# Cross attention of two transformer blocks: weights divided before or after the product, and the mask as a matmul or as an addition

## The chip, the cores and the metric

The kernel runs on one core of one Trainium2 chip. A core has five engines with queues of their own: TensorE (PE; PEld is its loading of weights), VectorE (DVE), ScalarE (ACT), GpSimd (POOL) and SyncE (SP, which issues most DMAs here). The metric is the device time of one execution in microseconds (us), lower is better. TensorE writes to PSUM, of which the kernel has eight banks of 128x512 float32; VectorE and ScalarE read it, and in this kernel GpSimd works on SBUF alone.

## What is computed

Two transformer blocks in float32, one after the other, on x of shape (2, 1024, 256), with a context of (2, 64, 256): 16 heads of 16, so the scores of the self attention are 1024 x 1024 per head and batch and those of the cross attention 1024 x 64. Block 0 ends in a mixture of eight experts of which each token takes two; block 1 ends in a plain feed-forward layer. Cut to what matters here:

```python
def _mha(q_in, kv_in, ...):                       # block 0, self and cross
    scores = jnp.einsum('bhqd,bhkd->bhqk', q, k) / jnp.sqrt(jnp.float32(dh))
    attn = jax.nn.softmax(scores, axis=-1)
    out = jnp.einsum('bhqk,bhkd->bhqd', attn, v)
...
# block 1, cross attention
attn = jnp.einsum('bhnd,bhmd->bhnm', q, k) * SCALE
bias = (1.0 - codebook_mask.astype(attn.dtype))[:, None, None, :] * -10000.0
attn = jax.nn.softmax(attn + bias, axis=-1)
ca = _merge(jnp.einsum('bhnm,bhmd->bhnd', attn, v)) @ ca_proj_w.T
```

Only block 1's cross attention has a mask. Blocks are called layers below.

## The kernel before

**The loop.** Self attention (`self_attention`, one call per layer) works head group by head group: a *cell* is one of 128 steps, with four heads at once on TensorE's four row groups. In a cell it makes four "a" scores (L805) whose row maxima VectorE reduces from PSUM (L812), ten cells ahead (`LEAD`), four "b" scores (L816) whose exponentials ScalarE writes to SBUF (L822), and, for cells one or two back, the product with the values (L867). Its result is copied by ScalarE (L876, L879) and added up by GpSimd (L880). With 128 cells and ten ahead, the maxima stop at cell 118; `maxima[0]` says whether they still run, and `helper()` gives GpSimd while they do and VectorE after.

**The planner.** Everything else is written as Python generators, run by `Stream`. A generator gives out instructions and yields: a positive number is a step's planned TensorE time, a number of zero or less a pause (0.0: until the next cell; -1.5: at least 1.5 us, rounded up to cells of `CELL` = 2.9 us). After each cell the loop takes steps as long as the planned time that is owed allows (`RATE`: 2.5 us a cell in layer 0, 1.1 in layer 1, more where deadlines ask for it). After the last cell `rest` runs what is left, by rank and by the pauses. So the order of each engine's queue is fixed when the program is built: what a step gives out stands in each queue behind the cell's own work.

**The cross attention.** Each layer has four *units* of 512 rows (n = 0 to 3). A unit becomes available when the self attention of its rows is projected, every 32 cells. It is normalised (`norm`), weighed (`weigh`), and then added to x (`share`). Unit n waits for unit n - 1. `weigh` first projects the queries (L1113, L1120). Then, for two halves g of the heads with four score tiles r each (a tile is 128 rows of 8 blocks of 64 keys):

- `scores(g, n)` makes two tiles in two banks (L1143). In layer 1 a matmul of one row, ones by the mask, opens each sum (L1134).
- While the maxima run, ScalarE copies the tile to SBUF (L1154), and later steps `largest` reduce the eight maxima on VectorE (L1163) and subtract them on GpSimd (L1164). After the maxima VectorE does both at once, from PSUM.
- `weights_turned` transposes two tiles (L1179), and ScalarE takes the exponential on the way out of PSUM (L1183).
- `product(g)` multiplies by the values (L1192), sums each head's exponentials with 16 small matmuls (L1202), copies the product to `q` (L1209) and inverts the sums (L1211).
- `divided(g)` spreads the inverses with four matmuls (L1217) and multiplies (L1224).

Which of two step lists a unit follows is read from `maxima[0]` once, after the query projection (L1230). The lists differ in the pauses.

In layer 0 a unit is followed by `dispatch_task`, which chooses experts on VectorE and sends rows with 8 indirect DMAs from GpSimd; the experts' slots (`Mixture`) run after the loop, from 650 to 890 us. In layer 1 units 0 and 1 are followed by `forward_norm`, and the feed-forward tasks run after the loop.

**Constants.** `picks` (768 columns) holds the 0/1 matrices of the sums: `O_SUM` has four blocks of 32 columns, one for each r.

Of the kernel before, what the change touches and what calls it, by code (L numbers as in the profile page):

```python
# [50 lines left out]
P = 128  # L51
# [52 lines left out]
NCOL = 139  # L104


O_SUM, O_HEAD = 0, 128

O_ROWS, O_PART = 640, 704
NPICK = 768  # L110

W_O, W_V, W_Q, W_K = 0, 512, 1024, 1536
NSELF = 2048
# [88 lines left out]
def two_blocks(  # L202
# [323 lines left out]
    def self_attention(layer, tail, heads, arrive, extra, when_ready, beside=None):  # L526
# [224 lines left out]
        def side_by_side(parts, dst):  # L751

            i, o = bank()
            j, s = bank()
            for half, part in enumerate(parts):
                nc.tensor.matmul(
                    o[64 * half : 64 * (half + 1), :], lhsT=picks[:, O_ROWS : O_ROWS + 64],
                    rhs=part, start=True, stop=True,
                )
            for half, part in enumerate(parts):  # L760
                for c in range(4):
                    nc.tensor.matmul(
                        s[32 * c : 32 * (c + 1), :P],
                        lhsT=picks[:, O_PART + 32 * half : O_PART + 32 * (half + 1)],
                        rhs=part[:, c * P : (c + 1) * P],
                        start=(half == 0),
                        stop=(half == 1),
                    )
            inv = small.tile([P, P], F32, tag="inv", name=f"inv_{names}", bufs=1)
            nc.vector.reciprocal(inv, s[:, :P])  # L770
            nc.scalar.copy(dst, o)
            free.extend((j, i))
            yield 1.5
            yield -1.6
            i, by = bank()
            for c in range(4):
                nc.tensor.matmul(
                    by[:, c * P : (c + 1) * P],
                    lhsT=picks[:, O_HEAD + c * P : O_HEAD + (c + 1) * P],
                    rhs=inv, start=True, stop=True,  # L780
                )
            nc.vector.tensor_tensor(dst, dst, by, ALU.mult)
            free.append(i)
            yield 0.55
            yield -1.0
# [72 lines left out]
        def product(cells):  # L858

            h = cells[0] // 8  # L860
            b, g = h // 8, h % 4
            for cell in cells:
                stream.until(("values", b, cell % 8 & 6))
            n, o = bank()
            for cell in cells:
                for j in range(4):
                    nc.tensor.matmul(  # L867
                        o[32 * j : 32 * j + VW, :],
                        lhsT=V[b][:, cell % 8, 4 * g + j, :],
                        rhs=exps.pop((cell, j)),  # L870
                        start=(cell == cells[0]),
                        stop=(cell == cells[-1]),
                    )
            if cells[0] % 8 == 0:
                acc[h] = opool.tile([P, 512], F32, tag="acc", name=f"acc_{names}{h}")
                nc.scalar.copy(acc[h], o)  # L876
            else:
                part = opool.tile([P, 512], F32, tag="part", name=f"part_{names}{cells[0]}")
                nc.scalar.copy(part, o)  # L879
                helper().tensor_tensor(acc[h], acc[h], part, ALU.add)  # L880
            free.append(n)
            if cells[-1] % 8 == TB - 1:
                at_cell(cells[-1] + 3, lambda: finish(h, cells[-1] + 3))
# [219 lines left out]
    def weigh(layer, b, pool, w, name, held):  # L1103
# [21 lines left out]
        shape = [P, 4 * 2, SK]  # L1125
        less, pts, whole_scores = {}, {}, set()

        def scores(g, n):

            got = [(r, *bank()) for r in (2 * n, 2 * n + 1)]  # L1130
            for t in range(4):
                for r, _, p in got if layer == 1 else ():
                    at = slice(32 * r, 32 * r + 1)
                    nc.tensor.matmul(  # L1134
                        p[:, t * P : (t + 1) * P].rearrange("p (u k) -> p u k", k=SK),
                        lhsT=ones[at, :],
                        rhs=mask_f[at, b * SK : (b + 1) * SK].unsqueeze(1).to_broadcast([1, 2, SK]),
                        start=True,
                        stop=False,
                    )  # L1140
                for r, _, p in got:
                    rows = slice(32 * r, 32 * r + 32)
                    nc.tensor.matmul(  # L1143
                        p[:, t * P : (t + 1) * P],
                        lhsT=q[rows, g, t * P : (t + 1) * P],
                        rhs=kbd[rows, g, b].rearrange("p u k -> p (u k)"),
                        start=(layer == 0),
                        stop=True,
                    )
            for r, i, p in got:  # L1150
                sc = less[g, r] = pool.tile([P, 512], F32, tag="sc", name=f"sc_{name}{g}{r}", bufs=4)
                if maxima[0]:

                    nc.scalar.copy(sc, p)  # L1154
                    whole_scores.add((g, r))
                else:
                    subtract(sc, p, nc.vector, f"{g}{r}")
                free.append(i)

        def subtract(sc, src, engine, tag):  # L1160
            src = src.rearrange("p (c k) -> p c k", k=SK)
# [4 lines left out]
                mx.unsqueeze(2).to_broadcast(shape), ALU.subtract,  # L1166
            )

        def largest(g, r):
            if (g, r) in whole_scores:  # L1170
                subtract(less[g, r], less[g, r], nc.gpsimd, f"{g}{r}")

        def weights_turned(g, n):

            for r in (2 * n, 2 * n + 1):
                i, p = bank()
                sc = less.pop((g, r))
                for t in range(4):
                    nc.tensor.transpose(  # L1179
                        p[:, t * P : (t + 1) * P], sc[:, t * P : (t + 1) * P], ident  # L1180
                    )
                pt = pts[g, r] = pool.tile([P, 512], F32, tag="p1", name=f"pt_{name}{g}{r}", bufs=4)
                nc.scalar.activation(pt, p, AF.Exp, scale=SCALE)  # L1183
                free.append(i)


        inverse = {}

        def product(g):
            i, o = bank()  # L1190
            for r in range(4):
                nc.tensor.matmul(  # L1192
# [7 lines left out]
            for r in range(4):  # L1200
                for c in range(4):
                    nc.tensor.matmul(  # L1202
                        s[32 * c : 32 * (c + 1), :P],
                        lhsT=picks[:, O_SUM + 32 * r : O_SUM + 32 * (r + 1)],
                        rhs=pts[g, r][:, c * P : (c + 1) * P],
                        start=(r == 0),
                        stop=(r == 3),
                    )
            nc.scalar.copy(q[:, g, :], o)  # L1209
            inv = inverse[g] = pool.tile([P, P], F32, tag="inv", name=f"inv_{name}{g}", bufs=2)  # L1210
            nc.vector.reciprocal(inv, s[:, :P])  # L1211
            free.extend((i, j))

        def divided(g):
            i, p = bank()
            for c in range(4):
                nc.tensor.matmul(  # L1217
# [6 lines left out]
            nc.vector.tensor_tensor(q[:, g, :], q[:, g, :], p, ALU.mult)  # L1224
            free.append(i)

        held.update(ot=q, divided=divided)
        cost = 1.9 if layer else 1.0
        SC, LA, TU, PR, DI = scores, largest, weights_turned, product, divided
        if maxima[0]:  # L1230

            for now, wait in (
                (((SC, 0, 0), (LA, 0, 0)), 0.0),
                (((LA, 0, 1),), 0.0),
                (((SC, 0, 1), (LA, 0, 2)), 0.0),
                (((TU, 0, 0), (LA, 0, 3)), 0.0),
                (((SC, 1, 0), (LA, 1, 0)), 0.0),
                (((TU, 0, 1), (LA, 1, 1)), 0.0),
                (((SC, 1, 1), (LA, 1, 2)), 0.0),
                (((PR, 0), (LA, 1, 3)), -1.5),  # L1240
                (((TU, 1, 0),), None),
                (((DI, 0), (TU, 1, 1)), -1.4),
                (((PR, 1),), None),
            ):
                for step, *args in now:
                    step(*args)
                us = sum({SC: cost, TU: 1.15, PR: 1.1, DI: 0.55}.get(step[0], 0.0) for step in now)
                if us:
                    yield us
                if maxima[0]:  # L1250
                    yield 0.0
                elif wait is not None:
                    yield wait
            return
        for step, *args, wait in (
            (SC, 0, 0, None),
# [1 line left out]
            (TU, 0, 0, None),  # L1258
            (SC, 1, 0, None),
            (TU, 0, 1, -1.3),  # L1260
            (PR, 0, None),
            (SC, 1, 1, None),
            (TU, 1, 0, None),
            (DI, 0, None),
            (TU, 1, 1, -1.6),
            (PR, 1, None),
        ):
            step(*args)
            yield {SC: cost, TU: 1.15, PR: 1.1, DI: 0.55}[step]
            if wait:  # L1270
                yield wait

    def share(w, name, first, held):

        yield -2.6
        held["divided"](1)
        yield 0.55
        yield -1.2
        for t0 in range(0, 4, 2):
            yield from project_task(held["ot"], w, first + t0, t0, 2)  # L1280
# [732 lines left out]
def _layout(inputs):  # L2013
# [81 lines left out]
    cols[:E, C_RB] = l0["router_b"]  # L2095

    picks = np.zeros((P, NPICK), f32)
    for r in range(4):
        for u in range(2):
            for c in range(4):  # L2100
                picks[SK * u : SK * (u + 1), O_SUM + 32 * r + 8 * c + 2 * r + u] = 1.0
    for j in range(4):
        for d in range(DH):
            picks[32 * j + d, O_ROWS + DH * j + d] = 1.0
# [49 lines left out]
```

## Time and profile before

| | |
|---|---|
| median of 4 runs | 1614.35 us (1608.72 to 1615.77) |
| the profiled execution | 1607.04 us, span 1605.3 us |
| granted TensorE clock, mean | 0.991 |
| maxima of layer 0 (L805) | 22.7 to 544.9 us, cells to about 585 us |
| maxima of layer 1 | 900.3 to 1406.5 us, cells to about 1446 us |
| query projections of the units, layer 0 (L1113) | from 247.2, 379.8, 523.6 and 616.4 us |
| query projections of the units, layer 1 | from 1146.4, 1300.6, 1421.8 and 1483.9 us |
| tiles copied at L1154 / reduced from PSUM at L1163 | 38 / 26 |

Busy time by stretch, in us, from the view of windows:

| stretch | us | PE | DVE | ACT | POOL |
|---|---|---|---|---|---|
| loop of layer 0, 64 to 545 | 481.0 | 473.8 | 364.4 | 336.4 | 168.3 |
| loop of layer 1, 947 to 1406.5 | 459.5 | 455.4 | 343.2 | 325.3 | 132.4 |
| last cells of layer 1, 1407 to 1446 | 39.0 | 36.9 | 18.6 | 31.5 | 6.3 |
| end, 1446 to 1601 | 155.0 | 153.9 | 44.3 | 43.1 | 10.9 |

How to read the lines further below: a line of the timeline is start, duration, engine, line of the program, operation, what it writes from what, shapes, and how many instructions are merged; a float32 matmul is two instructions. In square brackets stands idle time of that engine before, and what ended it. Matmuls are pipelined, so a time on TensorE is best taken from one start to the next.

### The profile page before, as it was taken

To read this page: it belongs to the slowest core of one execution; us is meant where nothing else is said; L and a number is where in the kernel's file an instruction comes from. 1 tells how busy PE (TensorE), PEld (TensorE's weight loads), DVE (VectorE), ACT (ScalarE), POOL (GpSimd) and SP (SyncE) were. 2 spreads that over 40 slices of the span, in tenths; PEclk is the share of its full clock that TensorE was granted. 3 is DMA by queue.
4 is the path that set the end of the run, shared out by engine and by line. 5 is a ranking of instruction groups with operands and counts; after the bars stand their busy time and mean duration, and the time that the engine had idled before them with its cause. 6 is when DMAs were issued, how large, how long until landed. Compare 5 with 4: busy or idle time off the path is not lost. (4 is left out here: it accounts for less than half of the span.)

```text
span 1605.3 us, 28322 instructions
## 1 busy us (share of the span) xinstructions
PE 1569.6 (98%) x10710; PEld 874.3 (54%) x10710; DVE 982.5 (61%) x2094; ACT 914.5 (57%) x1770; POOL 411.0 (26%) x546
## 2 busy tenths in 40 slices
PE   7999999999998999999999999999999999999998
PEld 4433444544543547888888653344444445446766
DVE  6787766677779647611114558876767767845400
ACT  3487767666666755333223338876776676684321
POOL 2243323135235203411112033411222322311000
PEclk9899999999999999999999999999999999999999
DMA  5235311101000115375656320101110002000000
GB/s 162 111 135 202 106 28 35 28 21 48 15 21 35 55 50 198 117 276 197 201 185 209 89 83 18 35 22 24 31 41 15 22 14 84 22 8 21 14 13 27
DMA packets 55752, 121.07 MB, mean 75 GB/s; under 512 B 12219, under 2 KB 26429, under 8 KB 55229
## 3 DMA queue, kind: packets, MB, share of 16 engines
q1 hardware_dynamic: 51772, 109.07, 21.0%
q0 software_dynamic: 3456, 9.51, 1.6%
q8 instruction: 86, 1.41, 0.3%
q10 hardware_dynamic: 384, 0.66, 0.2%
q14 instruction: 54, 0.43, 0.1%
HBM read 71.68 MB, written 38.88 MB: 69 GB/s over the span
## 5 line engine op out<-in xcount | busy, mean ns | idle before, releaser
L812 DVE TENSOR_REDUCE mx_s<-banks 128x1 f32<-128x512 f32 x1024 | 634.1, 681 | 204.8 <-PE banks L805 203.0
L822 ACT ACTIVATE pt_s<-banks 128x512 f32<-128x512 f32 x1024 | 532.8, 609 | 156.9 <-PE banks L805 123.5
L805 PE MATMUL banks<-KS,QS 16*128 16x512 f32 x2048 | 533.6, 629 | 2.9 <-ACT part_s L879 1.4
L816 PE MATMUL banks<-qb_s,KS 32*128 32x512 f32 x2048 | 516.0, 621 | 7.4 <-DVE qb_s L715 3.6
L880 POOL TENSOR_TENSOR acc_s<-acc_s,part_s 128x512 f32<-128x512 f32 x141 | 179.4, 1272 | 433.0 <-ACT part_s L879 432.2
L816 PEld LDWEIGHTS banks<-qb_s,KS 32*128 32x128 f32 x2048 | 180.6, 186 | 179.4 <-DVE mx_s L812 107.1
L867 PE MATMUL banks<-pt_s,v_s 128*20 128x512 f32 x2048 | 262.1, 603 | 1.5 <-DVE mx_s L812 1.0
L805 PEld LDWEIGHTS banks<-KS,QS 16*128 16x128 f32 x2048 | 200.2, 185 | 70.5 <-issue 32.5
L867 PEld LDWEIGHTS banks<-pt_s,v_s 128*20 128x20 f32 x2048 | 43.1, 99 | 185.0 <-ACT pt_s L822 129.4
L1686 PE MATMUL banks<-w_slot,h_s 128*128 128x256 f32 x640 | 143.1, 380 | 0.0
L1686 PEld LDWEIGHTS banks<-w_slot,h_s 128*128 128x128 f32 x640 | 120.6, 190 | 19.7 <-DVE mx_s L812 1.5
L879 ACT COPY part_s<-banks 128x512 f32<-128x512 f32 x155 | 92.7, 598 | 61.0 <-PE banks L867 51.6
L1695 DVE SCALAR_TENSOR_TENSOR ys<-banks,gate,b 128x256 f32<-128x256 f32 x40 | 19.3, 483 | 162.1 <-PE banks L1686 160.9
L1662 ACT ACTIVATE h_s<-banks,w_slot 128x256 f32<-128x256 f32 x104 | 43.7, 471 | 111.1 <-issue 64.0
L1656 PE MATMUL banks<-xsT,w_slot 128*128 128x256 f32 x416 | 95.4, 381 | 0.7 <-ACT xsT L376 0.7
L1701 POOL DMA_INDIRECT results<-ys,to x40 | 38.8, 969 | 222.2 <-DVE ys L1695 179.7
L1656 PEld LDWEIGHTS banks<-xsT,w_slot 128*128 128x128 f32 x416 | 77.4, 190 | 14.9 <-DVE mx_s L812 2.3
L1164 POOL TENSOR_TENSOR sc_c<-sc_c,mx_c 128x512 f32<-128x512 f32 x38 | 40.0, 1053 | 97.3 <-DVE mx_c L1163 97.0
L1819 ACT ACTIVATE h_f<-banks,w_ff 128x512 f32<-128x512 f32 x32 | 22.0, 687 | 73.9 <-PE banks L1816 73.9
L635 PE MATMUL banks<-xT_s,w_att 128*128 128x512 f32 x128 | 61.5, 615 | 0.0
L1828 PE MATMUL banks<-w_ff,h_f 128*128 128x256 f32 x256 | 57.3, 380 | 0.0
L1662 ACT ACTIVATE h_s<-banks,spare 128x256 f32<-128x256 f32 x56 | 23.4, 471 | 58.7 <-issue 30.4
(272 smaller groups left out, 1637.9 us busy)
## 6 DMA issues: line engine op xcount, KB each, us to landing
w_slot<-in_ff_w_dram SPq DMA_DIRECT2D x40, 576.0 KB
sorted_rows<-fill SPq DMA_DIRECT2D x36, 520.0 KB
w_slot<-in_ff_w_dram SPq DMA_DIRECT2D x26, 514.0 KB
whole<-acc_s SPq DMA_DIRECT2D x30, 256.0 KB
spare<-in_ff_w_dram SPq DMA_DIRECT2D x14, 514.0 KB
xs<-sorted_rows SPq DMA_DIRECT2D x20, 260.0 KB
y<-results SPq DMA_DIRECT2D x16, 256.0 KB
QS<-stq_s SPq DMA_DIRECT2D x124, 32.0 KB
```

What stands on the lines that cost most here:

```text
L635: nc.tensor.matmul(p, lhsT=w[:, at + k * D + pair * P : at + k * D + (pair + 1) * P], rhs=xT[b][:, k, blk * 512 : (blk + 1) * 512], start= ...
L805: nc.tensor.matmul(sc, lhsT=QS[h % 4][r, qc * P : (qc + 1) * P], rhs=K[r, kh * 512 : (kh + 1) * 512], start=True, stop=True,)
L812: return i, lambda: nc.vector.tensor_reduce(mx[h][:, qc, j, kh : kh + 1], sc, AX.X, ALU.max)
L816: nc.tensor.matmul(sc, lhsT=K[r, n * P : (n + 1) * P], rhs=QB[h][r, :], start=True, stop=True)
L822: nc.scalar.activation(pt, sc, AF.Exp, scale=SCALE)
L867: nc.tensor.matmul(o[32 * j : 32 * j + VW, :], lhsT=V[b][:, cell % 8, 4 * g + j, :], rhs=exps.pop((cell, j)), start=(cell == cells[0]), st ...
L879: nc.scalar.copy(part, o)
L880: helper().tensor_tensor(acc[h], acc[h], part, ALU.add)
L1656: nc.tensor.matmul(ph[:, n, :], lhsT=w[:, at : at + P], rhs=xT[:, k, :], start=(k == 0), stop=(k == 1),)
L1662: nc.scalar.activation(h1[:, f, :], ph[:, n, :], AF.Gelu, bias=w[:, W_B1 + f : W_B1 + f + 1])
L1686: nc.tensor.matmul(py, lhsT=h1[:, f, h * P : (h + 1) * P], rhs=w[:, f * D : (f + 1) * D], start=(f == 0), stop=(f == 7),)
L1828: nc.tensor.matmul(py[:, n, :], lhsT=h1[:, f, t * P : (t + 1) * P], rhs=w2[:, f * D : (f + 1) * D], start=(f == 0), stop=(f == 7),)
```

## The change

- Units that begin while the maxima run (`whole`) take the exponential in SBUF on ScalarE (`exponentials`), before the transposes; VectorE sums each head's 64 weights and inverts the sums (`divided`), and the helper multiplies the tile by them. ScalarE then only copies the transposed tile, and the product needs no division: the 16 sum matmuls, the four that spread, the reciprocal and the multiplication fall away for them, and so does the division that opens `share`.
- Their steps are laid into 19 cells in layer 0 and 21 in layer 1: tile k's scores in cell k (+4, or +5 in layer 1, for the second half), in layer 1 the mask there and the maximum a cell later, the exponential two cells after the maximum, the division one cell after that, the turning seven (eight) cells after the scores. A pause between cells is one cell.
- The other units keep the division after the product (`undivided`, `division`), with the sums read from fewer columns of `picks`.
- The matmul of the mask is gone. In a whole unit of layer 1 GpSimd adds the mask to the copied tile (`mask`); a tile made after the maxima gets it from VectorE, out of PSUM into SBUF, and maximum and subtraction then read that.
- The planned time of a score step is 1.0 in both layers (layer 1 had 1.9), that of a product without sums 0.55.
- Buffers: three instead of two for the partial products, the inverses move into buffers that the normalisation has, `picks` shrinks to 680 columns.

```diff
-O_SUM, O_HEAD = 0, 128
-O_ROWS, O_PART = 640, 704
-NPICK = 768
+O_SUM, O_HEAD = 512, 0
+O_ROWS, O_PART = 552, 616
+NPICK = 680
...
-                part = opool.tile([P, 512], F32, tag="part", name=f"part_{names}{cells[0]}")
+                part = opool.tile([P, 512], F32, tag="part", name=f"part_{names}{cells[0]}", bufs=3)
...
+        whole = maxima[0]
+
         def scores(g, n):
 
             got = [(r, *bank()) for r in (2 * n, 2 * n + 1)]
             for t in range(4):
-                for r, _, p in got if layer == 1 else ():
-                    at = slice(32 * r, 32 * r + 1)
-                    nc.tensor.matmul(
-                        p[:, t * P : (t + 1) * P].rearrange("p (u k) -> p u k", k=SK),
-                        lhsT=ones[at, :],
-                        rhs=mask_f[at, b * SK : (b + 1) * SK].unsqueeze(1).to_broadcast([1, 2, SK]),
-                        start=True,
-                        stop=False,
-                    )
...
-                    subtract(sc, p, nc.vector, f"{g}{r}")
+                    if layer == 1:
+                        add_mask(sc, p, nc.vector)
+                    subtract(sc, sc if layer == 1 else p, nc.vector, f"{g}{r}")
                 free.append(i)
+
+        def add_mask(sc, src, engine):
+            row = mask_f[:, b * SK : (b + 1) * SK].unsqueeze(1).to_broadcast(shape)
+            sc, src = [t.rearrange("p (c k) -> p c k", k=SK) for t in (sc, src)]
+            engine.tensor_tensor(sc, src, row, ALU.add)
...
+        def mask(g, r):
+            if (g, r) in whole_scores:
+                add_mask(less[g, r], less[g, r], nc.gpsimd)
+
...
+        def exponentials(g, r):
+            nc.scalar.activation(less[g, r], less[g, r], AF.Exp, scale=SCALE)
+
+        def divided(g, r):
+
+            sc = less[g, r].rearrange("p (c k) -> p c k", k=SK)
+            sm = pool.tile([P, 8], F32, tag="smc", name=f"sm_{name}{g}{r}", bufs=4)
+            nc.vector.tensor_reduce(sm, sc, AX.X, ALU.add)
+            nc.vector.reciprocal(sm, sm)
+            helper().tensor_tensor(sc, sc, sm.unsqueeze(2).to_broadcast(shape), ALU.mult)
...
-                nc.scalar.activation(pt, p, AF.Exp, scale=SCALE)
+                if whole:
+                    nc.scalar.copy(pt, p)
+                else:
+                    nc.scalar.activation(pt, p, AF.Exp, scale=SCALE)
...
+        if whole:
+
+            m = layer
+            cells = [[] for _ in range(19 + 2 * m)]
+            for k in range(8):
+                g, r = divmod(k, 4)
+                at = k + (4 + m) * g
+                if r % 2 == 0:
+                    cells[at].append((SC, g, r // 2))
+                    cells[at + 7 + m].append((TU, g, r // 2))
+                if m:
+                    cells[at].append((MA, g, r))
+                cells[at + m].append((LA, g, r))
+                cells[at + m + 2].append((EX, g, r))
+                cells[at + m + 3].append((DI, g, r))
+            for g in range(2):
+                cells[11 + m + (7 + m) * g].append((PR, g))
+            for now in cells:
                 for step, *args in now:
                     step(*args)
...
-                if maxima[0]:
-                    yield 0.0
-                elif wait is not None:
-                    yield wait
+                if now is not cells[-1]:
+                    yield 0.0 if maxima[0] else -1.5
             return
...
     def share(w, name, first, held):
 
-        yield -2.6
-        held["divided"](1)
-        yield 0.55
+        if held["division"]:
+            yield -2.6
+            held["division"](1)
+            yield 0.55
         yield -1.2
```

## The prediction

> **What bounds the kernel now.** I read the page first, then the groups by line, then the timeline of single stretches, and the same timeline again at the two last units of the cross attention.
>
> ```profile
> PE 1569.6 (98%) x10710; PEld 874.3 (54%) x10710; DVE 982.5 (61%) x2094; ACT 914.5 (57%) x1770; POOL 411.0 (26%) x546
> ```
>
> TensorE has a matmul in flight in 98% of the span, and the chain of waits runs along it. But its two attention loops (50 to 585 us and 938 to 1446 us) consist of 256 cells in which VectorE and ScalarE are nearly full too, so a cell has to be looked at by itself. A bare cell (four maxima scores, four exponential scores, one product):
>
> ```profile
> 99.49 0.70 PE L816 MATMUL banks<-qb_s,KS 32*128 32x512 f32 x2
> ...
> 100.70 2.06 ACT L822 ACTIVATE pt_s<-banks 128x512 f32<-128x512 f32 x4 [0.39 <-PE banks L805]
> 100.75 2.46 DVE L812 TENSOR_REDUCE mx_s<-banks 128x1 f32<-128x512 f32 x4
> ...
> 102.41 0.70 PE L816 MATMUL banks<-qb_s,KS 32*128 32x512 f32 x2
> ```
>
> The cell takes 102.41 - 99.49 = 2.92 us. Successive maxima start 2.46/4 = 0.6 us apart, successive exponentials 2.06/4 = 0.5 us apart (a single one reads 681 and 609 ns; neighbours overlap). So VectorE needs 2.4 of the 2.92 us and ScalarE, with the copy of the product, five times 0.5 = 2.5: each has 0.4 to 0.5 us to spare in a bare cell, more where TensorE has other work in it. What happens beyond that is seen where statistics crowd in:
>
> ```profile
> 452.31 0.70 PE L816 MATMUL banks<-qb_s,KS 32*128 32x512 f32 x2
> ...
> 454.64 4.95 DVE L812 TENSOR_REDUCE mx_s<-banks 128x1 f32<-128x512 f32 x8
> ...
> 455.75 0.70 PE L816 MATMUL banks<-qb_s,KS 32*128 32x512 f32 x2
> ```
>
> This cell has the four maxima and two statistics pairs (0.42 + 0.18 us each): some 1.2 us more on VectorE, and it takes 3.44 us, 0.52 us more. A cell with one pair (the bare one above has it) pays nothing. So the rule I use: TensorE sets the cell, up to about half a us of extra VectorE or ScalarE work is free, and what is beyond it is paid.
>
> **What is removed.** The steps of the cross attention, in layer 0 and at the end of layer 1:
>
> ```profile
> 619.90 1.72 PE L1143 MATMUL banks<-kbd,q_c 32*128 32x128 f32 x32
> 621.55 1.99 PE L1058 MATMUL banks<-w_ctx,kvT 128*128 128x256 f32 x8
> ...
> 1499.27 1.06 PE L1202 MATMUL banks<-pt_c,picks 128*32 128x128 f32 x32
> 1500.25 0.49 PE L1134 MATMUL banks<-mask_i,ones 1*128 1x128 f32 x4
> ...
> 1503.17 1.06 PE L1217 MATMUL banks<-inv_c,picks 128*128 128x128 f32 x8
> 1504.06 0.60 PE L1179 MATMUL banks<-ident,sc_c 128*128 128x128 f32 x4
> ```
>
> Two score steps without a mask advance TensorE by 621.55 - 619.90 = 1.65 us; the same two with the mask, in layer 1, run from 1487.41 to 1490.85, that is 3.44. A mask costs 0.9 us per step, and there are 16 such steps (4 units of layer 1, four each): 14.3 us. The 16 sums of a group take 1500.25 - 1499.27 = 0.98 us, the four matmuls that spread the inverse 1504.06 - 1503.17 = 0.89, so 1.87 us for each half of a unit that goes the new way.
>
> Which units do so is decided where the unit's projection ends, by whether the maxima are still running. The copies at L1154 tell: of 64 score tiles 38 took the copy, by time 8, 8 and 6 in layer 0 and 8 and 8 in layer 1. Units 0 to 2 of layer 0 and 0 and 1 of layer 1 therefore begin inside the maxima, five units or ten halves: 18.7 us. Layer 1's unit 2 begins at 1421.8, after the last maxima (1406.5), and stays with unit 3 on the old way, where VectorE adds the mask. Together 14.3 + 18.7 = 33.0 us leave TensorE's queue.
>
> **What is added to the five units.** Forty tiles, and for each:
> - ScalarE: an exponential from SBUF, while the one after the turning becomes a copy of equal price (598 against 612 ns). The trace has no 128x512 activation from SBUF; nearest are 0.48 (the spacing from PSUM) and 0.69 us (with a bias). I take 0.5, in a cell of its own: covered by the 0.4 to 0.5 us to spare; without cover 20 us in all.
> - VectorE: a sum like the maximum at L1163 (673 ns, 0.6 in a row) and a reciprocal of 128x8. The trace has 131 ns for 128x2 and 339 for 128x32; I take 0.18, on the line between. So 0.78 against the 0.5 to spare: 0.3 paid in a bare cell, 0 in one with a score, turning or product step, or with projections. In two cells of each half-pair the new sum meets a maximum: 0.6 + 0.78 - 0.5 = 0.9. Ten such cells, 9 us, and thirty others, some half of them bare, 4.5 us. Taken away on VectorE are the ten reciprocals (958 ns) and products (686), after which a cell's scores now advance TensorE by 2.20 instead of 1.93 us in the timeline: 2.7 us back. Some of the ten meet TensorE work that covers them; I take 6 us net, with bounds of 0 and 30 (forty times 0.78, nothing covered).
> - GpSimd: a product with a broadcast operand, like L1164's 1053 ns, and in layer 1 a mask, between that and the 1272 of L880; at most 24 + 32 = 56 more operations. A layer 1 cell with mask, subtraction and an accumulation has 3.4 us of GpSimd; its steps are called for one to two cells (3 to 7 us) later, so I price it at nothing. If it falls behind, the maximum waits for the mask and the exponential for the subtraction, both in order ahead of the next scores' drains. The third buffer for the partial products takes up some of the lag of the accumulation (ScalarE's copies waited 6.6 us for it in all); bounds -6 to +10.
>
> GpSimd's longer queue is also where a rule speaks against the change. A VectorE row first: the centring at L357 takes 405 ns beside an idle GpSimd and 748 on average when a GpSimd operation overlaps it. The Trainium skill, "SBUF — State Buffer", section "SBUF: two separate sides", says that the two engines hold a shared port pair exclusively, so that the loser is fully blocked, and names VectorE's two-port modes and its operations with two SBUF inputs. The trace agrees in kind. Should ten more centrings meet a GpSimd operation, the row makes it 3.4 us of VectorE time, most of it in the spare part; the rule, as an estimate from it, a whole GpSimd operation each, some 10 us.
>
> **What is moved.** A unit that took 12 to 14 cells in layer 0 is laid over 19, in layer 1 (some 20 to 23 before, since the planner's rate of 1.1 us a cell held it back) over 21. Its share, a project of 3.7 us, and in layer 0 the dispatch with its GpSimd DMAs follow some six cells later. Unit 2 of layer 0 then ends about when the loop does (585 us); unit 3 waits for the last project (595 us) anyway, and slot and context work stand beside it. SyncE's queue gets no new DMA. I price this at 0, between -8 (dispatch 1, whose cells 489 to 527 us lose some 10 us to VectorE, moves past the last maxima) and +8 (a starved start of the slots).
>
> **Units 2 and 3 of layer 1.** Their masks are 7.2 of the 14.3 us. VectorE's work on a tile grows from 1.33 (1489.57 to 1490.90, maximum and subtraction) by an addition of 0.6 to 0.7 to 2.0 us. In unit 3 the first two tiles would be ready at about 1492.7, but TensorE, 1.7 us earlier out of the scores and with one forward step of 1.8 us between, asks at 1491.0: 1.3 us of waiting after the transposes that can go ahead. The second pair waits 2.1 by the same walk, the last 2.2 instead of 0.6. That is 5 us for 3.6 saved. Unit 2 has loop cells beside it, or falls beside forward work like unit 3. I take 8 us for both, bounds 2 and 12.
>
> **Sum.** -33 + 6 + 8 = -19 us. The profiled execution took 1607.04 us (span 1605.3 and 1.7 around it), which makes 1588. It is 7.3 below the median of the runs, 1614.35; against that, **1595 us**. Its own range from the bounds is 1580 to 1608.
>
> **The rivals.**
> - *Drains set the cell (slower).* In the five units VectorE, not TensorE, ends the cell. Then their 25.9 us of removed matmuls return nothing, and 40 x 0.78 less the ten reciprocals and products (16.4) is paid: +15, with the tail at +1: 1630. It decides once the loss per tile passes (33 - 8)/40 = 0.6 us. For it: VectorE's 0.6 us steps fill 82% of a bare cell. Against it: 1.2 us more cost 0.52.
> - *Gain given back (no change).* Half of that loss, or GpSimd's order holding ScalarE in layer 1: about 1611. For it: each mask stands one cell ahead of a maximum. Against: GpSimd is 26% busy.
> - *Everything covered.* No stalls in the five units, dispatch past the maxima: -33 + 8 - 8, about 1581. For it: one statistics pair in a bare cell is free. Against: the cells of sum and maximum.
> - If the units chose their way otherwise than the copies suggest (layer 1's unit 2 reaching the maxima), 3.7 us of matmuls and 4 us of waits would change places: inside the range.
>
> **How the numbers follow.** Forecast 0.50, drains 0.20, given back 0.14, covered 0.16. Predicted is the forecast's 1595. Left out on each side is about a tenth: below 1574 and above 1626. A measurement here tells 0.3% (4.8 us) from no change. Faster takes the forecast, the covered case and a little of "given back": 0.68; within 0.3% most of "given back": 0.11; slower the drains: 0.21.
>
> **What would show it.** L1134 gone; L1202 and L1217 down from x512 and x128 to x192 and x48 (three of eight units); cells of the five units with 2.92 to 3.3 us where bare; the last maxima of layer 1 some 15 us earlier; more waiting of the turning at L1179 after 1440 us. Wrong would be the prediction if the scores in those units take over 2.5 us a cell, if the subtraction on GpSimd comes after the exponential is due, or if TensorE's busy share falls under 96% in the loops.

## The result and the profile after

The changed kernel takes 1616.14 us in the median of 47 runs (1611.54 to 1619.93), the kernel before 1612.4 beside it (72 runs, 1607.19 to 1618.04). The ratio is 1.0022 with a 95% interval of 1.0016 to 1.0028: 3.6 us longer where 19 less were forecast. The profiled execution has a span of 1610.0 us. The page's busy line and its slices of TensorE and of the granted clock:

```profile
PE 1550.0 (96%) x10054; PEld 843.4 (52%) x10054; DVE 1024.4 (64%) x2194; ACT 940.2 (58%) x1821; POOL 472.7 (29%) x589
...
PE   7999999999999888999999999999999999989898
...
PEclk9899999999999999999999999999999999999999
```

TensorE has a matmul in flight for 19.6 us less (the prediction took 33 us out of its queue), and the span is 4.7 us longer: its idle time has gone up by 24. The slices show where: three with an 8 where layer 0's loop ends and behind it (slices 14 to 16, 523 to 644 us), and two more near the end. The loops themselves went well. A bare cell in the timeline:

```profile
99.75 0.70 PE L817 MATMUL banks<-qb_s,KS 32*128 32x512 f32 x2
...
101.02 2.46 DVE L813 TENSOR_REDUCE mx_s<-banks 128x1 f32<-128x512 f32 x4
...
102.67 0.70 PE L817 MATMUL banks<-qb_s,KS 32*128 32x512 f32 x2
```

It is 2.92 us as before. The cross attention's steps, as the view of one group of tiles gives them (minimum, median and longest duration in ns, then first and last start):

```profile
L1235 PE MATMUL banks<-pt_c,picks x192: 272/273/273, 616.9 to 1512.2; 128*32 128x128 f32 x192
L1250 PE MATMUL banks<-inv_c,picks x48: 273/275/275, 620.1 to 1516.7; 128*128 128x128 f32 x48
...
L1186 DVE TENSOR_REDUCE sm_c<-sc_c x40: 625/675/680, 263.8 to 1400.0; 128x8 f32<-128x512 f32 x40
L1187 DVE RECIPROCAL sm_c<-sm_c x40: 202/203/204, 264.5 to 1400.7; 128x8 f32<-128x8 f32 x40
L1188 POOL TENSOR_TENSOR sc_c<-sc_c,sm_c x33: 1040/1044/1493, 265.6 to 1397.3; 128x512 f32<-128x512 f32 x33
```

192 sums and 48 spreads are left, so five units took the new way, the ones that the copies had told. The new reciprocal takes 203 ns (0.18 taken), the sum 675.

The span is now cut at four points: TensorE's exponential scores (L816, L817 after) of cell 0, of cell 118 and of cell 246 (about where each layer's maxima end; both loops have some nine cells more), the same scores of layer 1's first cell, 128, and the turn of slot 5's rows at L1661 (L1622 before), behind which layer 0's slots follow at one pace in both kernels.

| us | before | after | difference |
| --- | --- | --- | --- |
| loop of layer 0, cell 0 to 118 | 495.7 | 479.5 | -16.2 |
| tail of layer 0, to slot 5's turn | 156.9 | 175.0 | +18.1 |
| slots, to cell 128 | 235.5 | 235.5 | 0 |
| loop of layer 1, to cell 246 | 468.8 | 454.7 | -14.1 |
| rest, to the end | 198.2 | 215.0 | +16.8 |

Together the loops got 30.3 us shorter, more than the 25.9 us of matmuls that the prediction took out of the five units; part of layer 1's gain is work that now stands behind its loop, as the runs below show. The two tails gave back 34.9 us. (Below, a *turning* is the transposes of `weights_turned`, a unit's *share* the matmuls that add it to x, and the *tail* of layer 0 the second row of the table.) The windows over layer 0's tail, before and after (stretch; its length, then busy time and instructions of PE, PEld, DVE, ACT and POOL; granted clock, share of DMA, GB/s):

```profile
545.80:702.70 156.90, 153.00 (x1010) 109.28 (x1007) 84.64 (x297) 78.91 (x155) 36.59 (x39) 0.99 0.39 135
```

```profile
529.80:704.80 175.00, 156.09 (x944) 108.88 (x941) 102.03 (x345) 79.33 (x158) 42.63 (x45) 0.96 0.37 128
```

TensorE is idle for 18.9 us instead of 3.9, at a lower clock. Four of the gaps, and the start of unit 2's share, from the timeline of PE after:

```profile
575.45 0.63 PE L370 MATMUL banks<-ident,ctx 128*128 128x128 f32 x4 [2.81 <-DMA ctx<-in_ctx_dram]
...
582.29 3.62 PE L438 MATMUL banks<-w_att,q_c 128*128 128x256 f32 x16
...
591.09 0.76 PE L370 MATMUL banks<-ident,xn_c 128*128 128x128 f32 x4 [1.73 <-DVE xn_c L358]
...
636.90 1.30 PE L1661 MATMUL banks<-ident,xs 128*128 128x128 f32 x8 [1.83 <-DMA xs<-sorted_rows]
...
646.45 1.97 PE L370 MATMUL banks<-ident,xd_m 128*128 128x128 f32 x8 [4.52 <-DVE xd_m L1358]
```

TensorE asks for a context tile, for unit 3's norm, for slot rows and for dispatch 3 before they are there: it has run out of other work. The share in the kernel before:

```profile
571.31 1.99 PE L437 MATMUL banks<-w_att,q_c 128*128 128x256 f32 x8
```

So unit 2's share starts at 582.3 us instead of 571.3 although the loop's last cell starts 18 us earlier (560.9 against 579.2); dispatch 2 starts at 598.7 (589.5 before), and slots 1 and 2 are turned at 636.9 (634.4).

### The profile page after: what moved, and what is told of

Its sections match the earlier page's. It is cut to its first block, busy times and chain, and to the rows that moved or that the text cites. A ratio compares the mean times of both kernels' runs of the same rounds, so it can differ in the third digit from the quotient of the medians.

```text
span 1610.0 us, 27285 instructions
## 1 busy us (share of the span) xinstructions
PE 1550.0 (96%) x10054; PEld 843.4 (52%) x10054; DVE 1024.4 (64%) x2194; ACT 940.2 (58%) x1821; POOL 472.7 (29%) x589
## 5 line engine op out<-in xcount | busy, mean ns | idle before, releaser
L817 PE MATMUL banks<-qb_s,KS 32*128 32x512 f32 x2048 | 515.6, 622 | 8.3 <-DVE begin L1514 3.3
L881 POOL TENSOR_TENSOR acc_s<-acc_s,part_s 128x512 f32<-128x512 f32 x151 | 191.7, 1270 | 368.7 <-ACT part_s L880 367.7
L817 PEld LDWEIGHTS banks<-qb_s,KS 32*128 32x128 f32 x2048 | 178.8, 186 | 195.1 <-DVE mx_s L813 116.8
L868 PE MATMUL banks<-pt_s,v_s 128*20 128x512 f32 x2048 | 265.9, 604 | 2.6 <-DVE mx_s L813 1.9
L806 PEld LDWEIGHTS banks<-KS,QS 16*128 16x128 f32 x2048 | 198.3, 185 | 64.3 <-issue 28.7
L880 ACT COPY part_s<-banks 128x512 f32<-128x512 f32 x166 | 100.1, 603 | 45.4 <-PE banks L868 43.2
L1855 PE MATMUL banks<-hT_f,w_ff 128*128 128x512 f32 x128 | 58.4, 607 | 0.0
```

Of the source, the lines that this page charges most:

```text
L806: nc.tensor.matmul(sc, lhsT=QS[h % 4][r, qc * P : (qc + 1) * P], rhs=K[r, kh * 512 : (kh + 1) * 512], start=True, stop=True,)
L817: nc.tensor.matmul(sc, lhsT=K[r, n * P : (n + 1) * P], rhs=QB[h][r, :], start=True, stop=True)
L868: nc.tensor.matmul(o[32 * j : 32 * j + VW, :], lhsT=V[b][:, cell % 8, 4 * g + j, :], rhs=exps.pop((cell, j)), start=(cell == cells[0]), st ...
L1855: nc.tensor.matmul(ph, lhsT=w1[:, at : at + P], rhs=hT[:, k, :], start=(k == 0), stop=(k == 1))
```

## The experiments

Ratios are to the kernel before, run on the same chip: there it took 1613.9 us in the first four runs and 1628 to 1629 in the others, so ratios, not times, are compared across the groups. A ratio across the two paces is itself uncertain by some us: the loop of layer 0 takes the kernel before 495.7 us in the first profile and 505.7 at the slower pace, while kernels with three buffers and the new sums in units 0 and 1 take 479.5 to 482.0 at either, and the changed kernel itself was run at the faster pace alone. Stages of profiles are therefore given beside the ratios, and those of layer 0's tail are compared at one pace only.

| kernel | ratio | 95% interval |
| --- | --- | --- |
| changed kernel | 1.0022 | 1.0016 to 1.0028 |
| unit 2 of layer 0 on the old list | 0.9924 | 0.9905 to 0.9943 |
| matmul mask in units 2 and 3 of layer 1 | 0.9976 | 0.9962 to 0.9989 |
| both | 0.9878 | 0.9856 to 0.9900 |
| two buffers for the partial products | 1.0048 | 1.0027 to 1.0069 |
| no pauses in the long list | 0.9985 | 0.9973 to 0.9996 |
| unit 2 of layer 0 old, mask as bias in units 2 and 3 of layer 1 | 0.9841 | 0.9822 to 0.9859 |
| before, three buffers | 0.9944 | 0.9928 to 0.9960 |
| unit 2 of layer 0 and all of layer 1 old, mask as bias | 0.9836 | 0.9818 to 0.9854 |
| before again | 1.0010 | 0.9994 to 1.0026 |
| all units old, three buffers, mask as bias | 0.9902 | 0.9881 to 0.9924 |
| before, three buffers, unit 2 held back | 1.0054 | 1.0032 to 1.0076 |
| units 0 and 1 of layer 0 and unit 0 of layer 1 new, the rest old, mask as bias | 0.9785 | 0.9761 to 0.9810 |

**Unit 2 of layer 0 on the old list.**

```diff
-        whole = maxima[0]
+        whole = maxima[0] and name not in ("c02",)
...
+        if maxima[0] and not whole:
+            for now, wait in (
+                (((SC, 0, 0), (LA, 0, 0)), 0.0),
...
```

Behind it stand the eleven steps of the kernel before.

> The changed kernel, with layer 0's unit 2 alone on the old list of steps (11 cells, sums and spread matmuls instead of sums on VectorE). Theory T1 (unit 2's list of 19 cells, and its pauses of 1.5 us behind the last maxima, delay dispatch 2 and with it the slots that are to fill layer 0's tail): the tail from cell 118 to slot 5's turn falls from 175 us to about 157 to 162, unit 2's share starts by about 567 instead of 582.3 us, the 0.5 clock windows between 530 and 650 us go; 3.7 us of matmuls come back; together 10 to 14 us less than the changed kernel (ratio to the kernel before about 0.994 to 0.996). Rival R1 (the tail waits on the chain behind the last project and unit 3, whatever list unit 2 has): the tail stays at 172 to 177 and the time rises by the 3.7 us of matmuls. Rival R2 (only the clock loses it): PE idle in the tail unchanged at about 19 us.

The share starts at 562.8 us, dispatch 2 at 580.3, slots 1 and 2 are turned at 625.4, and the tail is 160.4 us (timeline of PE, then the window of the tail):

```profile
562.79 1.56 PE L438 MATMUL banks<-w_att,q_c 128*128 128x256 f32 x6
```

```profile
533.30:693.70 160.40, 153.39 (x1008) 108.03 (x1005) 92.86 (x327) 78.78 (x154) 41.58 (x45) 0.99 0.42 140
```

7 us of it idle. The ratio falls by 0.0098, 15.8 us at 1614 where T1 had 10 to 14, for one unit of eight, and although its 3.7 us of matmuls come back. T1 holds in its mechanism; R1 and R2 fall. One half-clock stretch is left at 542.8 us, where none was expected.

**The same lateness without the work.** In the kernel before, with three buffers and its own steps, unit 2 is only held back:

```diff
+            for _ in range(12 if name == "c02" else 0):
+                yield -1.5
```

> The kernel before with three buffers, in its own order, but layer 0's unit 2 held back by twelve pauses of 1.5 us at its end: nothing is added to VectorE, GpSimd or TensorE. Theory T1 (a late dispatch 2 alone takes the fill from layer 0's tail): share of unit 2 starts 8 to 18 us later, PE idle in the tail rises by 6 to 12 us, and the time by 8 to 16 us against 0.9944 (ratio 0.999 to 1.004). Rival R5 (it is VectorE's and GpSimd's extra work behind the loop, not the lateness): within 3 us of 0.9944.

The pauses cost more than their nominal 18 us: the share starts 59.2 us behind cell 118 instead of 25.5 (52.5 in the changed kernel). The ratio goes from 0.9944 to 1.0054, 17.9 us, where T1 had 8 to 16 for a smaller delay; the tail goes from 167.3 to 185.5 us, TensorE's idle time in it from 9.5 to 22.4, and the gaps of the changed kernel are back at the same places (timeline of PE):

```profile
593.37 1.08 PE L370 MATMUL banks<-ident,ctx 128*128 128x128 f32 x4 [4.66 <-DMA ctx<-in_ctx_dram]
...
637.11 0.50 PE L1465 MATMUL banks<-chosen_m,tri 128*128 128x32 f32 x2 [3.66 <-DVE chosen_m L1445]
...
669.03 1.39 PE L1695 MATMUL banks<-ident,xs 128*128 128x128 f32 x8 [2.79 <-DMA xs<-sorted_rows]
...
677.63 1.76 PE L370 MATMUL banks<-ident,xd_m 128*128 128x128 f32 x8 [3.54 <-DVE xd_m L1392]
```

Nothing was added to any engine, so lateness alone costs this much; R5 falls. Two waits of ScalarE that the last section describes stand in the tail of the kernel that it is compared with and not in this one, so 17.9 us is, if anything, too little.

**The long list without its pauses.**

```diff
-                if now is not cells[-1]:
-                    yield 0.0 if maxima[0] else -1.5
+                if now is not cells[-1] and maxima[0]:
+                    yield 0.0
```

> The changed kernel, but the long list's pauses of 1.5 us behind the last maxima are left out: layer 0's unit 2 sends the rest of its steps one behind the other, with the new arithmetic kept. Theory T1a (the pauses are what delays dispatch 2): share of unit 2 by about 568 us instead of 582.3, TensorE waits some 4 us inside the unit's last steps, the tail falls to about 163 us and the time by 8 to 12 us. Theory T1b (the 19 steps themselves, each behind VectorE and GpSimd, are what is long, and TensorE would then wait at the turnings): share before 575 us at the best, and the time within 4 us of the changed kernel. If neither mattered (R1 of the runs before): no change at all.

Between the two: the share starts at 566.7 us, as T1a has it, but TensorE meets GpSimd and VectorE at the turnings, as T1b has it (timeline of PE, then the window from 540 us):

```profile
539.98 1.00 PE L1196 MATMUL banks<-ident,sc_c 128*128 128x128 f32 x4 [3.59 <-POOL sc_c L1188]
...
554.12 1.09 PE L1196 MATMUL banks<-ident,sc_c 128*128 128x128 f32 x4 [2.60 <-DVE sc_c L1188]
```

```profile
540.00:564.00 24.00, 19.21 (x96) 10.62 (x100) 16.17 (x37) 10.88 (x20) 0.00 (x0) 0.50 0.00 1
```

Behind the first of these waits the clock stands at half for 23.9 us on end, and dispatch 2 comes at 593.2 us, 61.1 us behind cell 118, against 68.9 in the changed kernel and 47.0 with unit 2 on the old list. The tail is not T1a's 163 us:

```profile
532.10:716.50 184.40, 165.00 (x944) 113.10 (x941) 100.86 (x343) 81.85 (x160) 41.43 (x44) 0.90 0.36 121
```

That is 12.4 us more than the 172.0 of the run with the mask as bias below, which has unit 2 on the old list and the same pace. The ratio is 0.0037, 6 us, under the changed kernel's, but across the two paces, so a gain is not shown. Leaving out the pauses does not bring the tail back: begun five cells ahead of cell 118 (511.0 us in the changed kernel), 19 cells are too long with pauses or without, where the eleven steps begun in the same cell are not.

**The mask of layer 1's units 2 and 3, back as a matmul, and as a bias.**

```diff
+                for r, _, p in got if layer == 1 and not whole else ():
+                    at = slice(32 * r, 32 * r + 1)
+                    nc.tensor.matmul(
...
-                    if layer == 1:
-                        add_mask(sc, p, nc.vector)
```

> The changed kernel, with the mask of layer 1's units 2 and 3 put back into the scores as matmuls (VectorE adds no mask there). Theory T2 (VectorE's mask makes the turning late by more than the matmuls saved, and the gaps lower the clock): the waits of the turning fall by 8 to 11 us, 7.2 us of matmuls come back, the clock windows at 1431 and 1462 us go (3.4 us): 3 to 8 us less than the changed kernel. Rival R3 (the layer 1 tail loses its time to the work that moved into it from the loop, share, turning, product): 4 to 7 us more than the changed kernel.

7.4 us faster. In the changed kernel unit 2's timeline has VectorE at three operations a tile and TensorE behind them:

```profile
1440.00 0.68 DVE L1160 TENSOR_TENSOR sc_c<-banks,mask_i 128x512 f32<-128x512 f32 x1
...
1440.71 0.69 DVE L1165 TENSOR_REDUCE mx_c<-sc_c 128x8 f32<-128x512 f32 x1
1441.44 0.69 DVE L1166 TENSOR_TENSOR sc_c<-sc_c,mx_c 128x512 f32<-128x512 f32 x1
...
1442.18 0.66 PE L1196 MATMUL banks<-ident,sc_c 128*128 128x128 f32 x4 [1.36 <-DVE sc_c L1166]
...
1446.28 0.65 PE L1196 MATMUL banks<-ident,sc_c 128*128 128x128 f32 x4 [1.39 <-DVE sc_c L1166]
```

2.05 us from one addition to the next. With the matmul TensorE comes later and VectorE needs two operations; what TensorE's time advances by at the turnings (from the end of the matmul before to the end of each, summed from cell 246 on) falls from 21.1 to 11.1 us. T2 holds, R3 falls; of the two half-clock stretches that T2 expected to go, one stays (1436.5 us).

> Both of the above together. T1 and T2: the parts add, 13 to 22 us less than the changed kernel, ratio to the kernel before 0.987 to 0.994, faster than both kernels. R1 and R3: 8 to 11 us more than the changed kernel.

The parts add: -0.0144, 23.2 us. Then the mask as a bias: behind the turning a partition is a key, so the exponential can add it. It takes 688 ns in the median instead of 597, and neither TensorE nor VectorE has any work with the mask:

```diff
-                    nc.scalar.activation(pt, p, AF.Exp, scale=SCALE)
+                    nc.scalar.activation(
+                        pt, p, AF.Exp, scale=SCALE, bias=key_mask[:, b : b + 1]
+                    )
```

> Layer 0's unit 2 on the old list as in the first run, and the mask of layer 1's units 2 and 3 neither by matmul nor by VectorE: it is the bias of the exponential behind the turning, where a partition is a key (a column of 10000 times mask less the greatest mask of the row). Theory T2 (VectorE's addition ahead of the turning is what costs): the waits of the turning are as with the matmul mask, and 7.2 us of matmuls stay away: 6 to 8 us less than with both parts undone, about 1587 to 1589 us, ratio 0.982 to 0.985. Rival R4 (with the scores this short TensorE comes to the turning before VectorE is done even without the mask, 1.33 us per tile): half of it lost in waits, about 1591 to 1593.

0.0037 less than with the matmuls, 6.0 us; the rest from cell 246 is 203.7 us against 209.7, and the turnings advance TensorE by 12.3 us, nearly as with the matmuls (11.1): T2 holds, R4 falls. So the matmuls' 7.2 us are a gain where nothing replaces them ahead of the turning.

**The third buffer.**

> The changed kernel with two buffers for the partial products of the attention loops instead of three. Theory T4 (the third buffer gives the 3 us that the loop of layer 0 gains ahead of the first cross unit, cell 24): cell 24 starts 2 to 3 us later and the whole is 3 to 8 us slower than the changed kernel. Rival (the early gain is something else, the third buffer gives nothing): within 1 us of the changed kernel.

0.0026 slower, 4.2 us, and the loop of layer 0 5.8 us longer (485.3); cell 24 starts 3.4 us later. T4 holds. Alone, with the steps of the kernel before (the smaller `picks` and the moved buffers of the inverses are in this kernel too, and no run parts them from the third buffer):

```diff
-                part = opool.tile([P, 512], F32, tag="part", name=f"part_{names}{cells[0]}")
+                part = opool.tile([P, 512], F32, tag="part", name=f"part_{names}{cells[0]}", bufs=3)
```

> The kernel before in its own order of instructions, with three buffers for the partial products instead of two and nothing else of the change. Theory T4 (the third buffer alone shortens the loop of layer 0 by some 5 us): cell 118 some 5 us earlier counted from cell 0, ratio to the kernel before 0.995 to 0.998. Rival: 1.000 within its interval.

> The kernel before itself, profiled on the chip of the three runs beside it. Its stages should read as in the first profile (loop of layer 0 495.7 us from cell 0 to cell 118, tail to slot 5's turn 156.9, loop of layer 1 468.8, rest 198.2) plus what this chip and execution add; the ratio is 1.000 within its interval. What of the 0.56% that the third buffer alone gave shows as a stage is read against this one.

The kernel before comes to 1.0010 against itself, with three buffers to 0.9944, 9 us, a little more than T4 had. The view of the part tiles shows what went (what ended the idle time of the engine just before: us, times), first in the first profile of the kernel before, then with three buffers:

```profile
  POOL acc_s L880: 6.6, 3
```

```profile
  ACT part_s L880: 447.0, 110
  PE banks L868: 48.9, 59
  issue: 2.7, 6
```

ScalarE's waits for the accumulation are gone (6.6 us in three here, 6.2 in two in the profile of the kernel before at the slower pace), and at that pace the loop is 495.6 us against 505.7, with half clock (behind its start) for 13.7 instead of 27.3 us. Whether the clock was spared by the buffer or by chance is not shown: in the first profile of before, with two buffers, the loop had 10.2 us of half clock and took 495.7. That execution was on the good side; its 1607.04 us lie under all 72 other runs.

**The sums on VectorE, layer by layer.** The list of names in the first diff now takes in layer 1's units, or all.

> As the run with the mask as bias, but all four units of layer 1 take the old list, with sums and spreads by matmul and the mask as bias: in layer 1 nothing is left of the change but the missing mask matmuls. Theory T5 (in layer 1 sums on VectorE gain little: 7.5 us of sums and spreads in the loop against 5.9 us more waiting at its scores, and 6.4 us of the second unit moved into the tail): within 3 us of the run with the mask as bias. Rival (the sums' gain stands by itself): 6 to 8 us slower than that run.

> All units of both layers on the old list (sums and spreads by matmul), three buffers for the partial products, layer 1's mask as the bias of the exponential: of the change only the third buffer and the missing mask matmuls are left. From the runs so far: 0.9944 for the buffer, less 14.3 us (0.9%) of mask matmuls, is 0.9856. Theory T6 (the new sums in layer 0's units 0 and 1 gain 3 to 7 us of matmuls): 0.985 to 0.988, slower than the 0.9836 with the new sums there. Rival (the sums on VectorE gain nothing in layer 0 either): 0.982 to 0.984.

In layer 1 the new sums of two units give nothing that the runs can tell (0.9841 with, 0.9836 without). In layer 0 those of units 0 and 1 give 0.0066, 10.7 us, more than T6's 3 to 7.

By stages that is 17.1 us in the loop (497.5 to 480.4), of which 7.0 are lost again in the tail (165.1 to 172.1); the profiles differ by another 4.0 us ahead of cell 0 (58.0 and 54.0 us), where the new sums have no part, so the 10.7 us are no exact size. Of the 17.1 us, 7.7 are the sums and spreads themselves; the loop's own matmuls (scores and product) advance TensorE by 12.3 us less, helped by 6.8 us less of half clock, and other work by some 3 us more.

T6 had also started too low, at 0.9856: the kernel without new sums comes to 0.9902, so of the 14.3 us of mask matmuls only 6.8 came back by the ratio to before with three buffers (10.7 by layer 1's loop and rest, while cell 0 starts 5.4 us later than there).

Layer 1's loop and rest, with the new sums in units 0 and 1 and without:

```profile
943.00:1398.00 455.00, 450.46 (x3316) 191.17 (x3316) 349.21 (x618) 339.78 (x652) 174.12 (x193) 1.00 0.13 35
1398.00:1601.00 203.00, 194.18 (x1088) 122.20 (x1084) 72.67 (x163) 83.35 (x138) 21.25 (x51) 0.98 0.05 17
```

```profile
942.30:1412.30 470.00, 464.31 (x3528) 203.73 (x3528) 355.06 (x627) 337.22 (x642) 142.06 (x188) 1.00 0.12 34
1412.30:1599.00 186.70, 181.40 (x1037) 115.84 (x1036) 56.83 (x114) 72.57 (x121) 10.78 (x32) 1.00 0.05 18
```

With the new sums the loop is 15 us shorter and the rest 17 us longer. Unit 1's share (3.7 us), its last turnings and product, and unit 2's norm and projection fall behind the loop there.

> Layer 0's units 0 and 1 and layer 1's unit 0 on the new list, all others on the old one, layer 1's mask as the bias in units 1 to 3 (unit 0 keeps GpSimd's mask). T5 (sums on VectorE in layer 1 gain little even where nothing is pushed into the tail): within 2 us of 0.9836. Rival (only the second unit's late end spoils them): 3 to 4 us faster, 0.981 to 0.982.

0.9785, and 4.3 us less than the kernel without new sums in layer 1 over loop and rest (652.5 against 656.8; by the ratios, each known to 0.002, it is 8 us): the rival was right, and T5 wrong where unit 1 stays short. This kernel beats both: 1596.32 us where the kernel before took 1629.49.

## Why the prediction was wrong

The count behind the sum's first term, TensorE's 33 us, was right: 192 and 48 matmuls left, L1134's gone. What failed is the step **What is moved**, priced at 0: "Unit 2 of layer 0 then ends about when the loop does (585 us); unit 3 waits for the last project (595 us) anyway, and slot and context work stand beside it. ... I price this at 0, between -8 ... and +8". The unit did end there: its last product is at 579.5, its share at 582.3. But the loop that was to end with it ended some 18 us earlier, by the very gain that the other steps had forecast, and the slot and context work was not beside it: the slots are fed by the unit's share and dispatch, and the context work waited for its own DMA (2.81 us). I set the unit's new end against the old end of the loop. The upper bound had the mechanism, a starved start of the slots, at half its size. The runs give 15.8 us for it, or 19.5 in the terms of the sum, since the 3.7 us of matmuls that the unit saved went with it, and 18 for lateness alone. With the masks of layer 1's units 2 and 3 (14.6 against 8, below) added, these two terms missed by 26.1 us, by the ratios, where the sum missed by 22.6: the other terms together came out 3.5 us better than taken, with misses in both directions, which is luck.

The other steps:
- **Units 2 and 3 of layer 1.** The mechanism was right (2.0 us a tile, TensorE at the turning), its size not: 7.2 us saved and 7.4 lost makes 14.6 us of cost by the ratios (12.5 by the rest from cell 246, 215.0 against 209.7; 10.0 are seen at the turnings), against 8 taken and bounds of 2 to 12. The walk through unit 3 had the waits of the turning; not in it were unit 2, whose loop cells were gone by then, the work that came over from the loop, and the clock.
- **Drain stalls, +6.** In layer 0 they are below their lower bound of 0: two units took 7.7 us of matmuls out of the loop, and it got 17.1 us shorter. I had 2.7 us back from VectorE's reciprocals and products, for all five units; the runs don't part that from the clock. In layer 1, where GpSimd adds the mask, the loop's own matmuls advance by 3.7 us more with two new units than without.
- **The masks in layer 1's loop.** With old steps and no mask the loop takes 470.0 us (469.2 with it): of 8.3 us of matmuls, 4.7 went to work that moved in (norms, part of a projection) and 4.8, on balance, to the other matmuls, 2.9 of it to the maxima scores. The sum took the full 14.3 us for all masks. The gain is in the rest, 186.8 against 198.3.
- **Third buffer, inside "bounds -6 to +10".** Worth 4 to 9 us, and it should have stood in the sum: the 6.6 us of waits were read and not used.
- **The range.** The bounds named in the steps add up to -45 and +27 us, 1569 to 1641; the stated 1580 to 1608 is narrower than they are. The 1616 measured is inside them.
- **The rivals.** "Drains set the cell" is refuted by the loops. "Gain given back" has nearly the number (1611) and not the mechanism: little was lost inside the cells (the 3.7 us in layer 1). "Everything covered" counted on dispatch 1 past the last maxima; it came later (489.3 us against 468.2), and not past them. No rival had the tail of layer 0.
- **The wrongs named.** A bare cell stayed at 2.92 us, TensorE's share above 96% in both loops; the last maxima came 12 us earlier, not 15. The counts of matmuls and the waits at the turning behind 1440 us showed as listed. I looked for the failure inside the loops.

The Trainium skill, "TensorE: Matmul & The Clock Gate", section "Why this matters for your kernels", asks for no idle gaps of TensorE over about 3 us, since a window of idle brings the clock to half. It wasn't weighed in the prediction; the traces agree in kind and are stricter, as below.

## What to carry to other kernels

A step that is stretched to fit beside a loop has to end before the loop does, measured against the loop's new end, not its old one; and what is fed by it is not cover for it. Ask of each unit whether what it delays is the only work left behind the loop: the same change was worth 10.7 us in two early units and cost 15.8 in the last. Work for a slack engine pays inside the loop that has the slack; where it stands in a chain of its own (scores, mask, maximum, turning), a longer chain can cost more than the matmuls it saves, as it did here.

## Not expected of the hardware

- **Short gaps lower the clock.** Half clock comes in stretches of 3.41 us or multiples. I cut all fourteen traces into such windows, on a grid set by the first half-clock stretch, and left out the first 70 us: of 36 full-speed windows in which TensorE had a matmul in flight for less than 42% of the time, all were followed by half clock; between 42 and 61%, 24 of 60; between 61 and 80%, 9 of 131; above 80%, 3 of some 5900. A gap of 1.89 us (526.9 us in the changed kernel) was enough. The changed kernel has, between its start and its end, 27.3 us of half clock against 13.7 before. Once low it may stay: of 91 half-clock windows with TensorE busy over 97%, 26 were followed by another.
- **A ScalarE that waits for nothing seen.** At the pace at which the kernel before takes 1628 us, ScalarE sits idle twice in layer 0's tail, and the trace names no instruction of the core that released it (timeline of ACT, kernel before):

```profile
634.50 1.27 ACT L1120 ACTIVATE q_c<-banks,cols 128x512 f32<-128x512 f32 x2 [6.12 <-remote]
```

```profile
702.30 1.57 ACT L1662 ACTIVATE h_s<-banks,spare 128x256 f32<-128x256 f32 x4 [6.30 <-remote]
```

It costs TensorE 2.9 and 2.8 us, and half clock follows the second; that tail is 165.3 us there and 156.9 in the first profile. Seven of the eight profiles at this pace have both waits, that of unit 2 held back has neither, and none of the six at the faster pace has them. The record names chip 4 for runs of both paces, so the chip's number does not tell them apart. What ScalarE waits for stays open.
